# Four fused network layers: the feed-forward's last batch taken by tiles, and sums and boxes of the last stage laid out over its calls

## The chip, the cores and the metric

The kernel is one program on one core of a Trainium2 chip. The core has TensorE (PE in the profile; PEld is its weight load), VectorE (DVE), ScalarE (ACT), GpSimd (POOL), and SyncE (SP), which here only issues transfers. DRAM is reached by DMA from queues on SP, ACT and POOL. The metric is the time of one execution on the device in microseconds, the median of several runs. A measurement of this kernel spreads over some 0.2%. "Span" is the time from the first to the last event in a profiled execution.

## The reference, cut to what matters

The input x has 4 batches of 384 channels on 64 x 64 points. Four layers of the form x = x + layer(norm(x)) follow, where the norm takes groups of 12 channels. Layer 0 is attention, layer 1 a frequency-domain mix, layer 2 a gated block with convolutions and a feed-forward, and layer 3 a depthwise 7 x 7 convolution whose kernels are computed from the input. The change lies in the end of layer 2 and in layer 3:

```
# layer 2, end; _bn is a batch norm with statistics over batch and points
h1 = _gelu(_bn(_pw(tok, cm_w1), cm_g1, cm_b1))      # 384 -> 768 channels
h2 = _bn(_pw(h1, cm_w2), cm_g2, cm_b2)              # 768 -> 384
return gate * (tok + h2) + (1.0 - gate) * x
# layer 3
x_avg, x_max = x.mean(axis=(2, 3)), x.max(axis=(2, 3))
x_w = gelu(x_avg @ w_avg.T + b_avg + x_max @ w_max.T + b_max)
xr = (x_w[:, :, None] * w_mix[None]).reshape(b, c, 7, 7)
Gx = sqrt(sum(xr * xr)); Nx = Gx / (Gx.mean(axis=1) + EPS)
kern = gamma * (xr * Nx) + beta                     # one 7 x 7 kernel per batch and channel
out = depthwise_conv(x, kern)
```

Two facts shape the program. A batch norm needs the statistics of all batches before a single value can be used. And layer 3's kernel is a scalar per batch and channel times w_mix, plus beta everywhere. So the convolution splits into one with the fixed w_mix (weights as Toeplitz matrices, TensorE) and a sum over a 7 x 7 box (the "boxes"). The scalars, called a_s and b_s, need the mean, the largest value and the variance of the whole of layer 3's input (here "x2").

## The kernel before, in words

Channels lie in three tiles j of 128 partitions, and a batch's 4096 points are cut into four blocks or pieces of 1024. A scheduler at compile time puts the program's instructions in order on every engine: it starts from the order in which the Python code emits them, and lets an instruction go ahead if it is ready earlier by a cost model. At run time each engine works its list in order. So the place at which the code emits an instruction decides, but loosely. A named tile of a pool with `bufs=n` rotates over n buffers, and a writer waits until the buffer's last user is done.

**Feed-forward, first half** (lines 1643 to 1699). 768 hidden channels are computed, stored in DRAM (`hidden`), with statistics of each. The sum `wx` of all that x2 has besides h2 is stored too.

**Feed-forward, second half** (lines 1702 to 1739). For each batch b, block i (3 MB of `hidden` into `f_h`, two buffers, GELU in place on ScalarE, line 1722) and tile j, `feed_back` does 12 products of 512 columns (line 1758; every fp32 product is two records in the profile). It copies them out of PSUM on ScalarE (line 1765), takes statistics on DVE (line 1766), and, for j of 1 and 2, stores h2 in DRAM from a rotating buffer `f_h2` (line 1768, POOL's queue). Tile 0's h2 stays in SBUF in `z_`. The loop goes by batch, then block, then tile; only the last batch has one exchange: tile 0 of its last block comes one job sooner. When tile 0 is complete, `h2_norms` computes its factors `gh` and `g0`, and `x2_first` forms x2 = h2 * gh + wx for tile 0 (line 1812) in seven steps ahead of each of the remaining jobs. For batch 3 this is in `z_` with squares and maxima taken at once (lines 1825 and 1827); for batches 0 to 2 it is in three large buffers of 2 MB, `x2_ahead`, into which wx was loaded beforehand. After the last job `h2_norms` does tiles 1 and 2.

**Layer 3** (`phase_g`). `group_means` needs the norms of all tiles. `to_strips` turns tile 0 of x2 around (ScalarE and DVE scale, TensorE transposes in line 2061, ScalarE and DVE copy back in lines 2066 and 2068) into `z_`, all four batches. Then 48 calls of `conv7` follow, 16 for each tile, 8 channels each: four Toeplitz products on DVE or POOL (line 2117), 64 records of matmuls (line 2130) and a copy of the result, stored to `raw` (tiles 0 and 1, line 2145) or added to `rest` and stored to the output (tile 2, lines 2142 and 2147). Other work is cut into steps by Python generators, and a call of conv7, which has five yields, emits a few of them:

- `x2_later`: squares and maxima of tile 0's batches 0 to 2, put behind the strips by `issue_after`.
- `x2_of` (line 2030): x2 of tiles 1 and 2. For each of eight pairs (j, b) it loads 2 MB of wx into one of the same three large buffers, loads h2 by quarters (`g_h`), scales on ScalarE into PSUM with g0 as bias (line 2044), adds on DVE (line 2045), squares, takes the maximum, and stores 2 MB to DRAM. Five steps; two or three a call, all within the first 16 calls.
- `factors`: the chain to a_s and b_s, emitted in one go when tile 0 is convolved, behind all of x2.
- `half_strips`: the strips of the next tile, from DRAM.
- `boxes` (line 2150): for each of twelve pairs (j, b) four parts of three steps each. Sums on POOL and DVE, transposes (line 2208), matmuls (line 2243), the addition into x (line 2245). For tiles 0 and 1 `raw` comes back as `in_raw` (line 2218) and is added: for tile 0 through ScalarE with bias g0 (line 2226) and DVE (line 2229), for tile 1 in one DVE instruction (line 2224). Then the 2 MB of output are stored (line 2233). Tile 2's boxes go to `rest` (line 2235). One step at each of conv7's five yields in tile 1's calls, four or five in tile 2's.

## Time and profile before

| | us |
|---|---|
| median of 5 runs (4696.37 to 4707.07) | 4703.63 |
| the profiled execution's own time | 4706.53 |
| its span | 4704.7 |
| feed-forward, second half: matmuls of line 1758, first to last start | 3512.7 to 4009.1 |
| first convolution (line 2130) | 4051.7 |
| last square of x2 (line 1825) | 4254.4 |
| first box matmul (line 2243) | 4278.7 |
| last convolution ends | 4700.2 |

The page counts busy time of each engine, shows the span in 40 slices with the granted clock of TensorE and the share of time that the 16 DMA engines were busy, and lists groups of instructions by line: busy time, mean of one, idle time of the engine ahead of them and what ended it. A busy share over the whole span (TensorE has 4353.4 us, 93%) says little about the stages in question, so times by stage are used: rows that give, for a stretch, its length, the busy time and the number of instructions of TensorE, its weight load, DVE, ACT and POOL, then the clock, the DMA share and GB/s. A wait is listed as the engine and line that waited, what it waited for, the total in us, how often, and the longest.

### The profile page before, as it was taken

How to read it: one execution, taken by the hardware profiler on the slowest of the kernel's cores; microseconds unless marked ns; L12 is line 12 of the kernel's file. 1: busy time of each engine (PE TensorE's matmuls, PEld its weight loads, DVE VectorE, ACT ScalarE, POOL GpSimd, SP SyncE). 2: the span in 40 equal slices, each digit the busy share in tenths (PEclk: the TensorE clock that was granted, in tenths of full speed). 3: DMA queues.
4: the chain of work that ended last, by engine and by line, in shares of the span. 5: the costliest groups of instructions: out<-in, count | busy, mean ns of one | idle time of the engine just before them, and what ended most of it. 6: DMA issues, size and time to landing. Idle time of an engine off the chain costs nothing. (4 is left out here: it accounts for less than half of the span.)

```text
span 4704.7 us, 49708 instructions
## 1 busy us (share of the span) xinstructions
PE 4353.4 (93%) x18445; PEld 2419.2 (51%) x18445; DVE 2848.9 (61%) x4673; ACT 1966.6 (42%) x2915; POOL 806.3 (17%) x756
## 2 busy tenths in 40 slices
PE   7899999999999999998988999699999999678898
PEld 2233444334443444444548888344444444578888
DVE  6766566645666456545877788655531112867788
ACT  3444344444444444434535666311123333664431
POOL 1000000000000000000025566000000000236665
PEclk9999999999999999998989999799999999888999
DMA  4311222121111211112328999876764333696787
GB/s 138 114 33 50 83 67 74 46 70 47 54 67 56 69 34 61 54 61 82 125 90 290 316 336 325 280 260 246 262 235 161 127 143 136 254 361 229 243 270 260
DMA packets 282128, 730.35 MB, mean 155 GB/s; under 512 B 22059, under 2 KB 122518, under 8 KB 269974
## 3 DMA queue, kind: packets, MB, share of 16 engines
q1 hardware_dynamic: 211336, 407.56, 27.3%
q0 software_dynamic: 38448, 173.96, 9.9%
q10 hardware_dynamic: 32094, 145.57, 7.7%
q8 instruction: 149, 2.44, 0.2%
q14 instruction: 101, 0.83, 0.1%
HBM read 433.13 MB, written 293.86 MB: 155 GB/s over the span
## 5 line engine op out<-in xcount | busy, mean ns | idle before, releaser
L822 ACT ACTIVATE probs<-sc_s 128x1024 f32<-128x1024 f32 x512 | 496.7, 1020 | 689.6 <-PE av L932 588.2
L932 PE MATMUL av<-probs,vt 128*128 128x512 f32 x1536 | 714.9, 602 | 0.0
L1137 DVE SCALAR_TENSOR_TENSOR acc<-band,vecs,acc 128x512 f32<-128x512 f32 x708 | 496.2, 745 | 44.7 <-POOL band L1096 39.6
L1758 PE MATMUL h_m<-f_h,cm_w_t 128*128 128x512 f32 x1152 | 497.0, 594 | 7.4 <-ACT f_h L1722 7.4
L1424 PE MATMUL conv_m<-toep,z 128*128 128x192 f32 (+1 forms) x2304 | 446.7, 351 | 21.7 <-DVE z L1353 12.0
L932 PEld LDWEIGHTS av<-probs,vt 128*128 128x128 f32 x1536 | 275.6, 191 | 338.1 <-issue 334.4
L2130 PE MATMUL conv_m<-toep,z 128*128 128x128 f32 x3072 | 387.9, 284 | 44.7 <-DVE toep L2117 36.2
L1424 PEld LDWEIGHTS conv_m<-toep,z 128*128 128x128 f32 x2304 | 402.6, 194 | 45.7 <-ACT d_o L1435 15.6
L2130 PEld LDWEIGHTS conv_m<-toep,z 128*128 128x128 f32 x3072 | 374.1, 200 | 46.9 <-issue 22.5
L1670 PE MATMUL h_s<-e_tok,cm_w_t 128*128 128x512 f32 x768 | 362.7, 595 | 4.1 <-DVE e_tok L1655 4.1
L1758 PEld LDWEIGHTS h_m<-f_h,cm_w_t 128*128 128x128 f32 x1152 | 219.7, 191 | 284.8 <-issue 274.9
L814 PE MATMUL sc_s<-q,k 32*128 32x512 f32 x2048 | 307.5, 643 | 15.9 <-ACT probs L822 15.6
L1405 POOL TENSOR_TENSOR toep<-w,band 128x1280 f32<-128x1280 f32 x96 | 278.2, 2898 | 200.2 <-PE conv_m L1424 187.8
L1058 PE MATMUL t_m<-w_in_t,xb 128*128 128x384 f32 x768 | 278.4, 497 | 4.6 <-DVE coef L1075 4.4
L968 PE MATMUL proj_m<-xm,w_proj_t 128*128 128x512 f32 x576 | 271.8, 611 | 6.4 <-DVE xm L907 4.9
L1677 ACT COPY e_h<-h_s 128x1024 f32<-128x1024 f32 x96 | 97.2, 1012 | 399.5 <-PE h_s L1670 399.5
L1679 DVE BATCH_NORM_STATS2 h_st<-e_h 128x6 f32<-128x512 f32 x192 | 123.5, 685 | 213.4 <-ACT e_h L1677 213.3
L1670 PEld LDWEIGHTS h_s<-e_tok,cm_w_t 128*128 128x128 f32 x768 | 146.3, 191 | 187.9 <-issue 183.2
L1058 PEld LDWEIGHTS t_m<-w_in_t,xb 128*128 128x128 f32 x768 | 142.7, 192 | 141.6 <-issue 58.8
L975 DVE SCALAR_TENSOR_TENSOR x_res<-proj_m,bn_c,x_res 128x512 f32<-128x512 f32 x96 | 71.8, 748 | 236.4 <-PE proj_m L968 236.2
L1766 DVE BATCH_NORM_STATS2 h_st<-f_h 128x6 f32<-128x512 f32 x64 | 44.2, 693 | 260.7 <-ACT f_h L1765 260.7
L1670 PE MATMUL h_s<-z,cm_w_t 128*128 128x512 f32 x384 | 196.1, 592 | 0.0
(459 smaller groups left out, 6368.3 us busy)
## 6 DMA issues: line engine op xcount, KB each, us to landing
d<-d_o ACTq DMA_DIRECT2D x48, 1024.0 KB
c_d<-d SPq DMA_DIRECT2D x48, 1024.0 KB
hid<-e_h ACTq DMA_DIRECT2D x16, 3072.0 KB
f_h<-hid SPq DMA_DIRECT2D x16, 3072.0 KB
x_in<-in_x SPq DMA_DIRECT2D x96, 256.0 KB
x_res<-in_x SPq DMA_DIRECT2D x32, 768.0 KB
xa<-x_res POOLq DMA_DIRECT2D x32, 768.0 KB, 3.9
xa_out<-xa SPq DMA_DIRECT2D x32, 768.0 KB
```

What stands on the lines that cost most here:

```text
L814: nc.tensor.matmul(s[:, g], lhsT=k4[32 * g : 32 * g + 32, c], rhs=q[i][32 * g : 32 * g + 32], start=True, stop=True,)
L822: nc.scalar.activation(p[:, h * 1024 : (h + 1) * 1024], s[:, 2 * h : 2 * h + 2].rearrange("p a b -> p (a b)"), AF.Exp, scale=0.25,)
L932: nc.tensor.matmul(av[0], lhsT=vt[:, 4 * c + v, :], rhs=p[:, v * 512 : (v + 1) * 512], start=c == 0 and v == 0, stop=c == 7 and v == 3,)
L968: nc.tensor.matmul(m, lhsT=self.w_proj[:, j, o * P : (o + 1) * P], rhs=xm[:, j], start=j == 0, stop=j == NJ - 1,)
L1058: nc.tensor.matmul(m[:, 0:C], lhsT=xb[:, j], rhs=self.w_in[:, j, :], start=j == 0, stop=j == NJ - 1,)
L1137: nc.vector.scalar_tensor_tensor(out, src(j, k), w, done, ALU.mult, ALU.add)
L1405: eng.tensor_tensor(t, self.w53[:, at : at + 160].rearrange("p (m n) -> p m n", n=8).unsqueeze(2).to_broadcast([P, 20, 8, 8]), band.rearra ...
L1424: nc.tensor.matmul(m[:, c * 256 + to : c * 256 + to + 64 * (k1 - k0)], lhsT=self.z_[:, at : at + P], rhs=t[:, 10 * c + k0 : 10 * c + k1].r ...
L1670: nc.tensor.matmul(s[:, v, :], lhsT=w1[:, j, o * P : (o + 1) * P], rhs=t[j][:, v * 512 : (v + 1) * 512], start=j == 0, stop=j == NJ - 1,)
L1679: nc.vector.bn_stats(st[:, o, 8 * b + 2 * i + v, :], h[:, o, v * 512 : (v + 1) * 512])
L1758: nc.tensor.matmul(m, lhsT=w2[:, o, j * P : (j + 1) * P], rhs=h[:, o, v * 512 : (v + 1) * 512], start=o == 0, stop=o == 5,)
L2130: nc.tensor.matmul(m[:, ch % 4 * P : (ch % 4 + 1) * P], lhsT=self.z_[:, at : at + P], rhs=t[:, 8 * c + 2 * i : 8 * c + 2 * i + 2].rearrang ...
```

## The change

The last batch's loop in the feed-forward goes by tile first: all four blocks of tile 0, then of tile 1, then of tile 2. For this all four blocks of its hidden values must be in SBUF: blocks 0 and 1 (12 pieces) go to the three large buffers `x2_ahead`, blocks 2 and 3 to the two buffers of `f_h`. So tile 0's norms come eight jobs ahead of the end. `x2_first` then forms x2 of tile 0 for all batches in `z_`, loading wx by pieces into three small buffers and a spare, with squares (into PSUM) and maxima at once, and stores each batch. Norms of tile 1 follow before the last four jobs, and `x2_second` forms x2 of tile 1, batch 0. When the large buffers have served as hidden values, ScalarE copies tile 0's batches 0 to 2 from `z_` into them (12 copies). `f_h2` has two buffers instead of three.

In layer 3 `x2_later` is gone. `x2_of` has seven pairs, two steps a call, and `factors`, cut by three yields, comes as the last piece of the same list; only when this list is empty do the boxes start, one step at each yield of conv7, through the end. g0 is left out of x2 of tile 1 (bias zero), as it was for tile 0, and the boxes of tile 1 add it through ScalarE like those of tile 0.

```diff
--- before.py
+++ after.py
-            jobs = [(b, i, j) for b in range(B) for i in range(4) for j in range(NJ)]
-            jobs[-4:-3], jobs[-3:-2] = jobs[-3:-2], jobs[-4:-3]
-            tiles, own = {}, iter(())
-            for b, i, j in jobs:
+            tiles = {}
+            def ready(b, i):
+                src = self.hidden[b][:, :, blk].rearrange("o p n -> p o n")
+                if b == B - 1 and i < 2:
+                    h, runs = [], ((0, 4), (4, 2)) if i == 0 else ((0, 2), (2, 4))
+                    for o0, n in runs:
+                        k = 6 * i + o0
+                        t = self.x2_ahead[k // 4][:, k % 4 * 1024 : (k % 4 + n) * 1024].rearrange("p (o n) -> p o n", o=n)
+                        nc.sync.dma_start(t, src[:, o0 : o0 + n])
+                        h += [t[:, o] for o in range(n)]
+                else:
+                    t = hp.tile([P, 6, 1024], F32, tag="h", name="f_h")
+                    nc.sync.dma_start(t, src)
+                    h = [t[:, o] for o in range(6)]
+                for o in range(6):
+                    self.last_gelu = nc.scalar.activation(
+                        h[o], h[o], AF.Gelu, bias=c1[:, o : o + 1], scale=a1[:, o : o + 1]
+                    )
+                tiles[b, i] = h
+            late = B - 1
+            for b in range(late):
+                for i in range(4):
+                    ready(b, i)
+                    if b == late - 1 and i > 1:
+                        ready(late, i - 2)
+                    if b == late - 1 and i == 3:
+                        ready(late, 2)
+                    for j in range(NJ):
+                        self.feed_back(b, i, j, w2, tiles[b, i])
+                    if (b, i) == (0, 0):
+                        self.mix_norms()
+            ready(late, 3)
+            self.ln_exp(self.last_gelu)
+            own = iter(())
+            for j in range(NJ):
+                for i in range(4):
+                    self.feed_back(late, i, j, w2, tiles[late, i])
+                    for _ in range(8):
+                        next(own, None)
+                    if j == NJ - 1 and i < 2:
+                        for b in range(1) if i == 0 else range(1, NJ):
+                            for q in range(4):
+                                at = q * 1024
+                                nc.scalar.copy(
+                                    self.x2_ahead[b][:, at : at + 1024], self.z_[:, b * N + at : b * N + at + 1024]
+                                )
+                self.h2_norms(slice(j, j + 1))
                 if j == 0:
-                    h = hp.tile([P, 6, 1024], F32, tag="h", name="f_h")
-                    tiles[b, i] = h
-                    nc.sync.dma_start(h, self.hidden[b][:, :, blk].rearrange("o p n -> p o n"))
-                    for o in range(6):
-                        last = nc.scalar.activation(
-                            h[:, o, :], h[:, o, :], AF.Gelu, bias=c1[:, o : o + 1], scale=a1[:, o : o + 1]
-                        )
-                    if b == B - 1 and i == 3:
-                        self.ln_exp(last)
-                    if b == B - 1 and 0 < i:
-                        nc.sync.dma_start(self.x2_ahead[i - 1], self.wx[i - 1][:, 0])
-                if (b, i, j) == (0, 1, 0):
-                    self.mix_norms()
-                for _ in range(7):
-                    next(own, None)
-                self.feed_back(b, i, j, w2, tiles[b, i])
-                if (b, i, j) == (B - 1, 3, 0):
-                    self.h2_norms(slice(0, 1))
-                    own = self.x2_first()
+                    first2 = self.x2_first()
+                    own = self.in_turn(first2, self.x2_second())
+                if j == 1:
+                    for _ in first2:
+                        pass
             for _ in own:
                 pass
-            self.h2_norms(slice(1, NJ))
+    def in_turn(self, *pieces):
+        for p in pieces:
+            yield from p
...
-        out = self.io.tile([P, 1024], F32, tag="x", name="f_h2") if j else self.z_[:, at : at + 1024]
+        out = self.io.tile([P, 1024], F32, tag="x", name="f_h2", bufs=2) if j else self.z_[:, at : at + 1024]
...
-            if j:
+            if j == NJ - 1:
-            if j == 0:
+            if j < NJ - 1:
...
     def x2_first(self):
-        for b in (B - 1, 0, 1, 2):
+        for b in range(B):
-                h = self.z_[:, b * N + at : b * N + at + 1024]
-                if b == B - 1:
-                    x = h
-                    other = spare if q % 2 else self.io.tile([P, 1024], F32, tag="wx", name="f_wx", bufs=1)
-                    nc.sync.dma_start(other, self.wx[b][:, 0, at : at + 1024])
-                else:
-                    x = other = self.x2_ahead[b][:, at : at + 1024]
-                nc.vector.scalar_tensor_tensor(x, h, self.gh[:, 0, b : b + 1], other, ALU.mult, ALU.add)
+                x = self.z_[:, b * N + at : b * N + at + 1024]
+                w = self.spare() if q == 3 else self.io.tile([P, 1024], F32, tag="wx", name="f_wx", bufs=3)
+                nc.sync.dma_start(w, self.wx[b][:, 0, at : at + 1024])
+                nc.vector.scalar_tensor_tensor(x, x, self.gh[:, 0, b : b + 1], w, ALU.mult, ALU.add)
                 yield
-                if b == B - 1:
-                    self.x2_piece(0, b, q, x, other)
-                    yield
-            nc.gpsimd.dma_start(self.scratch["x2"][b][0], self.x2_tile(b))
-    def x2_piece(self, j, b, q, x, junk, behind=()):
+                self.x2_piece(0, b, q, x, self.ps("x2_sq").rearrange("p a b -> p (a b)"))
+                yield
+            nc.gpsimd.dma_start(self.scratch["x2"][b][0], self.z_[:, b * N : b * N + N])
+    def x2_second(self):
+        nc = self.nc
+        for b in range(1):
+            for q in range(4):
+                sl = slice(q * 1024, q * 1024 + 1024)
+                x = self.io.tile([P, 1024], F32, tag="wx", name="f_wx", bufs=3)
+                nc.sync.dma_start(x, self.wx[b][:, 1, sl])
+                h = self.spare() if q % 2 else self.io.tile([P, 1024], F32, tag="x", name="f_h2", bufs=2)
+                nc.sync.dma_start(h, self.h2[b][:, 1, sl])
+                nc.vector.scalar_tensor_tensor(x, h, self.gh[:, 1, b : b + 1], x, ALU.mult, ALU.add)
+                yield
+                self.x2_piece(1, b, q, x, self.ps("x2_sq").rearrange("p a b -> p (a b)"))
+                nc.gpsimd.dma_start(self.scratch["x2"][b][1][:, sl], x)
+                yield
-        order = [self.tc.issue_after(e.ins) for e in behind] or [nullcontext()] * 2
-        with order[0]:
-            self.nc.scalar.activation(junk, x, AF.Square, bias=at(self.neg2), accum_out=to(self.x2_var))
-        with order[1]:
-            self.nc.vector.tensor_reduce(to(self.x2_max), x, AX.X, ALU.max)
-    def x2_later(self):
-        for b in range(B - 1):
-            for q in range(4):
-                junk = self.gw_p.tile([P, 1024], F32, tag="w7", name="x2_sq", bufs=3)
-                self.x2_piece(0, b, q, self.x2_tile(b)[:, q * 1024 : q * 1024 + 1024], junk, self.strip_ends)
-                yield
+        self.nc.scalar.activation(junk, x, AF.Square, bias=at(self.neg2), accum_out=to(self.x2_var))
+        self.nc.vector.tensor_reduce(to(self.x2_max), x, AX.X, ALU.max)
...
+            self.zero = cp.tile([P, 1], F32, tag="zero", name="zero")
+            nc.gpsimd.memset(self.zero, 0.0)
...
-            later = self.x2_later()
-            x2 = others(*(self.x2_of(j, b) for j in (1, 2) for b in range(B)))
-            boxes = others(*(self.boxes(j, b) for j, b in ((2, 0), (2, 1), (2, 2), (2, 3), (0, 0), (0, 1), (0, 2), (0, 3))))
-            boxes1 = others(*(self.boxes(1, b) for b in range(B)))
+            x2 = [self.x2_of(j, b) for j, b in ((1, 1), (1, 2), (1, 3), (2, 0), (2, 1), (2, 2), (2, 3))]
+            x2 = self.in_turn(*x2, self.factors())
+            boxes = self.in_turn(*(self.boxes(j, b) for j in (2, 0) for b in range(B)))
+            boxes1 = self.in_turn(*(self.boxes(1, b) for b in range(B)))
             self.load_mix(0)
+            x2_left = True
...
                         for k, _ in enumerate(self.conv7(j, 64 * half + 8 * n)):
                             if k == 0:
                                 next(strips, None)
-                            next(later, None)
-                            if j == 0 and (k < 2 or k == 2 and n % 2):
-                                next(x2, None)
-                            if j == 1 or j == 2 and (k or n % 2):
+                            if x2_left:
+                                if k < 2:
+                                    x2_left = next(x2, "none") != "none"
+                            else:
                                 next(boxes, None)
-                if j == 0:
-                    for _ in x2:
-                        pass
-                    self.factors()
-                    self.pair_scales(2)
                 if j == 1:
-                    boxes = others(boxes, boxes1)
+                    boxes = self.in_turn(boxes, boxes1)
...
-        nc.vector.tensor_sub(self.s_b[:, 0], self.g0[:, 0], m[:, 0])
-        nc.vector.tensor_scalar(self.s_b[:, 1:NJ], m[:, 1:NJ], -1.0, None, ALU.mult)
+        nc.vector.tensor_sub(self.s_b[:, 0:2], self.g0[:, 0:2], m[:, 0:2])
+        nc.vector.tensor_scalar(self.s_b[:, 2:NJ], m[:, 2:NJ], -1.0, None, ALU.mult)
...
+        yield
...
-        nc.vector.tensor_add(mx[:, 0], mx[:, 0], self.g0[:, 0])
+        nc.vector.tensor_add(mx[:, 0:2], mx[:, 0:2], self.g0[:, 0:2])
+        yield
...
+        yield
...
+        self.pair_scales(2)
...
+        bias = at(self.g0) if j == NJ - 1 else self.zero
...
-                nc.scalar.activation(m, h[:, v * 512 : v * 512 + 512], AF.Identity, bias=at(self.g0), scale=at(self.gh))
+                nc.scalar.activation(m, h[:, v * 512 : v * 512 + 512], AF.Identity, bias=bias, scale=at(self.gh))
...
-                if j:
-                    nc.vector.scalar_tensor_tensor(xp, d, self.a_s[:, j, b : b + 1], xp, ALU.mult, ALU.add)
-                else:
-                    nc.scalar.activation(
-                        d, d, AF.Identity, bias=self.g0[:, j, b : b + 1], scale=self.a_s[:, j, b : b + 1]
-                    )
-                    nc.vector.tensor_add(xp, xp, d)
+                nc.scalar.activation(d, d, AF.Identity, bias=self.g0[:, j, b : b + 1], scale=self.a_s[:, j, b : b + 1])
+                nc.vector.tensor_add(xp, xp, d)
```

## The prediction, made before the result was known

> **What bounds the kernel now.** I read the page first: the 40 slices, then the costliest groups. After that I read busy time by stage, the waits inside one stage, and the groups of the lines that the change touches.
>
> The page's span and four of its slice rows (a slice is 117.6 us):
>
> ```profile
> span 4704.7 us, 49708 instructions
> PE   7899999999999999998988999699999999678898
> DVE  6766566645666456545877788655531112867788
> PEclk9999999999999999998989999799999999888999
> DMA  4311222121111211112328999876764333696787
> ```
>
> The reader is to see TensorE at 9 in slices 31 to 34 (the feed-forward), where DVE is at 1 and 2 and DMA at 3. Slices 35 and 36 follow, where TensorE falls to 6 and 7, its clock to 8 and DMA rises to 9. The stages the change touches, one row each: end of the feed-forward, strips of tile 0, x2 with the first convolution, the factors, second third, last third.
>
> ```profile
> core 0: us, PE busy (x) PEld busy (x) DVE busy (x) ACT busy (x) POOL busy (x), PEclk, DMA share, GB/s
> 3886.00:4010.00 124.00, 123.70 (x289) 54.47 (x287) 41.25 (x62) 41.10 (x54) 5.84 (x11) 1.00 0.43 161
> 4010.00:4052.00 42.00, 21.46 (x137) 16.92 (x138) 34.16 (x66) 28.24 (x33) 12.71 (x29) 0.84 0.42 151
> 4052.00:4254.00 202.00, 149.51 (x1186) 146.62 (x1184) 147.29 (x162) 130.28 (x204) 74.95 (x60) 0.87 0.95 343
> 4254.00:4285.00 31.00, 23.14 (x132) 22.80 (x133) 20.03 (x47) 8.95 (x17) 15.34 (x20) 0.61 0.59 215
> 4285.00:4498.00 213.00, 190.07 (x1603) 186.41 (x1603) 165.65 (x211) 87.45 (x132) 141.60 (x135) 0.96 0.75 230
> 4498.00:4705.00 207.00, 186.78 (x1615) 184.06 (x1614) 182.25 (x229) 47.55 (x75) 119.61 (x105) 0.98 0.81 265
> ```
>
> So there are four different limits. The feed-forward is TensorE alone (123.7 of 124). The x2 stage is transfers (share 0.95, 343 GB/s). The factors stage is a chain of short operations, with the clock at 0.61. The last two thirds have TensorE at 89 to 90%, and in the last one DVE has 182 of 207. The waits inside 4051 to 4270 confirm the second:
>
> ```profile
> ACT x_m L2044 <- DMA g_h<-h: 47.5, 18, 6.5
> DVE x L2045 <- ACT x_m L2044: 40.6, 16, 6.5
> PE conv_m L2130 <- DVE toep L2117: 33.2, 8, 10.2
> POOL toep L2117 <- DMA wmix<-in_mix_t: 25.9, 5, 7.3
> ```
>
> ScalarE waits for h2 from DRAM, DVE for ScalarE, and the Toeplitz products behind those adds on DVE reach TensorE late.
>
> Prices:
>
> ```profile
> L1758 PE MATMUL h_m<-f_h,cm_w_t 128*128 128x512 f32 x1152 | 497.0, 594 | 7.4 <-ACT f_h L1722 7.4
> L1812 DVE SCALAR_TENSOR_TENSOR x<-z,gh,x 128x1024 f32<-128x1024 f32 x12 | 14.6, 1271 | 0.0
> L1827 DVE TENSOR_REDUCE x_max<-x 128x1 f32<-128x1024 f32 x44 | 52.6, 1212 | 0.0
> L2224 DVE SCALAR_TENSOR_TENSOR in_x<-in_raw,a_s,in_x 128x1024 f32<-128x1024 f32 x16 | 25.0, 1562 | 7.8 <-DMA in_raw<-raw 7.8
> L2226 ACT ACTIVATE in_raw<-in_raw,g,a_s 128x1024 f32<-128x1024 f32 x16 | 19.9, 1242 | 25.8 <-DMA in_raw<-raw 25.8
> ```
>
> **The change, part by part.** "Piece" means 1024 columns of one tile and batch.
>
> *Feed-forward, order.* The matmuls stay: 1152 records in 497.0 us, 10.3 us per call of feed_back (24 records of 0.43 us). A late block's 3 MB load took 12.6 us from issue (3947.97) to its first GELU, and its six GELUs 7.4 us. Blocks 0 and 1 go to idle buffers and can load at any time. Block 3 is issued when block (2,3) is done and first needed three calls (31 us) later, so 20 us are hidden: 0 us. Without that cover a late block would cost up to 20 us.
>
> *Feed-forward, added work.* Tile 0 ends 8 calls, 82 us, before the end. Into these go 16 + 4 pieces. On DVE each costs 1.27 + 1.21: 20 x 2.48 = 50 us, plus 16 x 0.69 for bn_stats, 61 of 82. On ScalarE there are 20 squares. The row into SBUF has 1.14 + 0.19; into PSUM it is bounded by two halves of the 0.77 us that L2044 takes there, 1.55. I take 1.2 (nearest in size), 28 us. Then 12 copies, between 1.01 (L1677, from PSUM) and 1.24 (L1374, SBUF), 14 us at 1.15, and 16 evacuations of 0.58: 51 of 82. Transfers: h2 4.2 MB, wx of tile 0 8.4, x2 of tile 0 8.4, the quarter 2.1 x 3: 27 MB in 82 us is 333 GB/s, against 343 above, so they fit with little to spare. Half of it is uneven: during tile 1 (41 us) DVE needs 45 us and transfers 19 MB, 55 us at 343, so that some 14 us spill into tile 2, which has 41 us and needs 15 of DVE. POOL's queue carries eight more stores, and h2's stores stand behind those that wait for DVE; f_h2 loses a buffer (3 to 2). Both hold an evacuation back; four PSUM buffers of 5.15 us and two f_h2 of 10.3 cover 41 us. So 0 us; ends -3 (below) and +20, if the spill outlasts tile 2.
>
> The Trainium skill (DMA: Bandwidth & Descriptors, "Issuing engines are not separate DMA queues") speaks against this move: starting transfers from several engines saves only issue time, since they share 16 engines. The same page's fabric ceiling of 435 GB/s would make the 19 MB 44 us, an estimate, and the spill 3 us instead of 14; no stretch here reached it.
>
> *Transition.* Now the last bn_stats starts at 4011.03, behind L1812, though its copy ended 4010.3; two tiles' norms follow until 4016.3. The strips start on ScalarE at 4020.3, when the last h2 store lands (issued 4011.9 behind a 2 MB store of x2, landed 4020.2). With x2 stored earlier and one tile's norms, I put the store's landing at 4018 (its median 7.7 us) and s_b at 4016.5. The strips themselves (30 us, ScalarE) stay. First convolution at 4049 instead of 4051.7: -2.7.
>
> *x2 stage.* Twelve squares and maxima of x2_later go (16 us ScalarE, 14.5 DVE), x2_of falls from 8 to 7, at 6.3 MB each. The first loads of x2_of no longer wait for x2_later's squares to free their buffer: wx was first issued at 4058.4; now at some 4028, bringing 3.7 MB ahead of 4049. Pieces go 2 to a call of conv7, so 28 pieces and their 7 stores end at call 17.5. Until then the transfers are 44.0 - 3.7, plus 17.5 x 0.79 (raw and wmix), strips of tile 1 some 5, one box load 2.1: 61 MB, at 350 GB/s (71 MB in 202 us now) 174 us. Against that TensorE has 17.5 x 64 records x 0.112 plus strips, some 135, DVE some 130. So x2 ends at 4223 rather than 4254.
>
> *Factors.* Three yields set them between calls. Now TensorE spent 31 us at 4254 to 4285 on one and a half calls. After: 1.7 calls at 7.15 us of matmuls and strips, some 12 us. Boxes start at 4235, with call 20 ahead, against 4285 with call 18 ahead. Ends: 4225, 4260 (the stall kept whole).
>
> *Second and last third.* From there 28 calls hold all 144 steps of the boxes, 5 a call; now 30 calls did. Calls 20 to 31: TensorE now has 190.1 us for 14 calls; less two calls (14.3) and 6.7 box parts (at 2.65 us, some 18) 158, at 92% 172 us. Calls 32 to 47 take 27 box parts, now 20. A part costs DVE 1.1 + 2 x 0.74 + 1.56 + 0.60 + 0.70 + 0.34 = 5.8, so 182 + 40 = 222 us, and at the 92% that DVE had in its best 50 us (46.0 busy, the row below) 241 us. TensorE has 205 there: DVE becomes the bound.
> ```profile
> 4600.00:4650.00 50.00, 43.77 (x373) 43.17 (x372) 46.02 (x60) 6.91 (x13) 32.30 (x29) 0.97 0.85 298
> ```
>
> For tile 1, L2224 gives way to L2226 and L2229: DVE equal (1.21 to 1.52 against 1.29 to 1.56), ScalarE 16 x 1.24 = 20 us more, beside only 47.6 busy of 207; its cost is a hop of 1.3 us per part, 0 while DVE has other work. Spreading leaves no spare step, so the last box's sums and its 2 MB store come after the last convolution: 7.9 us to land, as the last of now (4694.2 to 4702.1), where the present end has 0.5 MB.
>
> *Sum.* 4235 + 172 + 241 + 8 = 4656, against the profiled span of 4704.7 (its own time 4706.5, 1.8 around it, 2.9 above the median 4703.6). The difference, -49, on the median: 4655.
>
> **Rivals.**
> Better: DVE doesn't bind, and the 346 us of TensorE work left at 4235 run at the present 90.5%: 382 + 11, from 4225: 4618 in span, 4617. For it: 420 us held 348 of DVE without trouble. Against it: DVE's 92% in 4600 to 4650.
> The early pace stays: calls 0 to 15 took 11.6 us each now (4051.7 to 4237.5). If transfers keep that for 20 calls, boxes start at 4281, and the end comes 46 us later than forecast: 4702 in span, 4701. For it: the strips of tile 1 join the same engines at share 0.95. Against it: 61 MB rather than 71.
> Slower: DVE in the last third works at the share of the second, 78% (165.7 of 213), or less, since in_raw then passes ScalarE first and DVE, in order, waits with Toeplitz products behind. At 78%: 222 / 0.78 = 285, +44, 4699. It turns slower beyond +49, that is below 76.5%; at 72%, 308, 4722. For it: L2229 waited 13.9 us in four places. Against it: 88% in this third now.
> The change does not do what it says: x2 in the feed-forward stalls TensorE by the 20 us above: 4675, still faster.
>
> **How the numbers follow.** 0.2% is 9.4 us, about what a measurement here can tell from no change. Forecast 0.53, of it 0.08 for the stall of 20, own range 4630 to 4680; better 0.21; early pace 0.15; slower 0.11. Faster: 0.53 + 0.21 + 0.05 of the early pace = 0.79; same 0.06, all early pace; slower 0.11 + 0.04 = 0.15. From 4602 (15 under the better case) to 4702 (the early pace) some 0.8 is held.
>
> **What would show it.** Right: TensorE without gaps up to its last h_m; first conv_m within 4 us of 4049; g_h pieces 28, the last by 4225; no stretch of 25 us with the clock near 0.6; box steps spread to the end, DVE over 90% in the last third, a 2 MB store as the last transfer. Wrong: idle time before L1758; the wait for g_h not below 40 us; Toeplitz products late after call 32.

## The result and the profile after

The changed kernel takes 4713.79 us in the median, the kernel before 4704.82, taken alternately on the same chips. The ratio is 1.0015 with a 95% interval of 1.0008 to 1.0022: some 7 us slower, where 4655 us and a gain of 49 were forecast. The time lies above the range given (4630 to 4680).

The profiled execution's own time is 4712.19 us. From the page of the changed kernel, its span and four slice rows (a slice is 117.8 us):

```profile
span 4710.4 us, 49815 instructions
PE   7899999999999999998988899699999999789887
DVE  6766566645566446545877888655531115767787
PEclk9999999999999999998989999799999999889899
DMA  4301212121111111112338999776764335886776
```

VectorE has more work in the feed-forward's last slice (slice 34 at 5, where it was 2). But TensorE ends with 9, 8, 8, 7 where it had 8, 8, 9, 8: time was won in the middle and lost at the end. The stretches of the changed kernel: feed-forward's last part, strips, x2 until its last piece, the factors until call 20, calls 20 to 31, calls 32 to 47 (columns as in the prediction):

```profile
core 0: us, PE busy (x) PEld busy (x) DVE busy (x) ACT busy (x) POOL busy (x), PEclk, DMA share, GB/s
3880.00:4005.00 125.00, 123.58 (x288) 54.34 (x287) 68.33 (x101) 58.24 (x88) 8.99 (x17) 1.00 0.60 227
4005.00:4044.00 39.00, 24.49 (x136) 19.73 (x137) 31.22 (x56) 28.69 (x32) 12.48 (x29) 0.78 0.73 264
4044.00:4228.00 184.00, 152.58 (x1225) 150.09 (x1225) 129.45 (x140) 109.97 (x170) 76.98 (x62) 0.92 0.91 319
4228.00:4264.00 36.00, 32.59 (x229) 32.26 (x228) 22.80 (x43) 12.85 (x20) 15.21 (x16) 0.80 0.67 213
4264.00:4443.00 179.00, 160.14 (x1337) 157.52 (x1337) 131.18 (x171) 66.33 (x104) 116.07 (x115) 0.93 0.63 194
4443.00:4695.00 252.00, 210.71 (x1728) 205.75 (x1726) 206.00 (x267) 79.07 (x108) 135.86 (x125) 0.94 0.76 249
```

The reader is to see three things. In the feed-forward the added VectorE and ScalarE work costs TensorE nothing (123.58 of 125). The x2 stage has transfers at 0.91 and 319 GB/s, less than the 0.95 and 343 of before. And in the last row neither engine is full: VectorE 206 of 252 us (82%), TensorE 84%, where 92% of VectorE was forecast. What stands still there is told by the waits of calls 32 to 47:

```profile
ACT in_raw L2254 <- DMA in_raw<-raw: 67.6, 21, 8.5
PE box_m L2269 <- ACT ht L2241: 35.5, 12, 6.8
DVE in_x L2271 <- PE box_m L2269: 35.2, 15, 7.4
```

ScalarE waits for the transfer in_raw (67.6 us in 21 places), TensorE's box sums wait for ScalarE's copies ht, and VectorE's in_x waits for those sums.

Counted from the first convolution, which takes out how long the stages in front happened to take in a profile, the end comes after 666.6 us; before it was 653.0. So the loss lies behind the first convolution.

### The profile page after: what moved, and what is told of

It is laid out like the page before. It is cut to its first block, busy times and chain, and to the rows that moved or that the text cites. A ratio compares the mean times of both kernels' runs of the same rounds, so it can differ in the third digit from the quotient of the medians.

```text
span 4710.4 us, 49815 instructions
## 1 busy us (share of the span) xinstructions
PE 4365.2 (93%) x18445; PEld 2428.4 (52%) x18445; DVE 2849.9 (61%) x4680; ACT 1991.6 (42%) x2937; POOL 802.9 (17%) x760
## 5 line engine op out<-in xcount | busy, mean ns | idle before, releaser
L1791 PE MATMUL h_m<-f_h,cm_w_t 128*128 128x512 f32 x1008 | 436.4, 595 | 7.4 <-ACT f_h L1728 7.4
L1791 PEld LDWEIGHTS h_m<-f_h,cm_w_t 128*128 128x128 f32 x1008 | 192.5, 191 | 250.8 <-issue 240.0
L968 PEld LDWEIGHTS proj_m<-xm,w_proj_t 128*128 128x128 f32 x576 | 110.5, 195 | 159.5 <-issue 139.1
```

Source lines behind the costliest of these rows:

```text
L968: nc.tensor.matmul(m, lhsT=self.w_proj[:, j, o * P : (o + 1) * P], rhs=xm[:, j], start=j == 0, stop=j == NJ - 1,)
L1791: nc.tensor.matmul(m, lhsT=w2[:, o, j * P : (j + 1) * P], rhs=h[o][:, v * 512 : (v + 1) * 512], start=o == 0, stop=o == 5,)
```

## Experiments

Ratios are to the kernel before, with 95% intervals; a difference of two ratios is turned into us at 4705, and with intervals of this width such a difference is uncertain by 7 to 11 us. A profile is one execution, which can lie some us off the median of its kernel.

### One part at a time

Four kernels split the change into three parts: the feed-forward, the hop (tile 1's raw result through ScalarE) and the spreading (x2 at two steps per call, factors with yields, then boxes at five steps per call).

**Changed kernel without the hop.**

```
# g0 of tile 1 is in x2 again (bias of x2_of, x2_second, s_b, maximum), and
-                nc.scalar.activation(d, d, AF.Identity, bias=self.g0[...], scale=self.a_s[...])
-                nc.vector.tensor_add(xp, xp, d)
+                if j:
+                    nc.vector.scalar_tensor_tensor(xp, d, self.a_s[...], xp, ALU.mult, ALU.add)
+                else: ...   # as it was
```

> The changed kernel, but the raw result of tile 1 is added in one VectorE instruction as before the change (g0 of tile 1 goes into x2 again, in ScalarE's bias where x2 is formed in the convolution stage, and in 4 more ScalarE passes in the feed-forward's last stretch). Theory H (the hop: ScalarE waits for the transfer in_raw at the head of its list, the box transposes' copies ht stand behind it, TensorE's box sums wait for those and VectorE's in_x for these): ScalarE's waits on in_raw in the last third fall from 67.6 us to under 35, TensorE's waits of box_m on ht from 37 to about 20, and the time from 4714 to about 4690 (4680 to 4700). Theory S (the spreading: all box steps run in calls 20 to 47 at five per call with none to spare, at the pace that the conv and box work of one call have together): the waits change places, the time stays at 4706 to 4716.

4698.9 us, 0.9981 (0.9968 to 0.9994): 16 us off the changed kernel, at the slow edge of theory H's range. Its waits came as H said: in calls 32 to 47 ScalarE waits 28.9 us for in_raw (67.6 with the hop), TensorE's box sums 14.6 us for the copies ht (35.5). S is not refuted, since it may hold beside H.

**Feed-forward part alone.**

```
-            x2 = self.in_turn(*x2, self.factors())
+            x2 = self.in_turn(*x2)
...
+                            if j == 0 and (k < 2 or k == 2 and n % 2):
+                                next(x2, None)
+                            if j == 1 or j == 2 and (k or n % 2):
+                                next(boxes, None)
...  # factors in one block after call 15; no hop, as in the run above
```

> The feed-forward part of the change alone: last batch by tiles, two blocks in large buffers, x2 of tile 0 and the first batch of tile 1 formed there; but tile 1's raw result added in one VectorE instruction, the factors in one block after call 15 and the boxes at five and 4.5 steps per call from call 16 on, all as in the kernel before. x2 is then formed by call 14, so nothing of it is left at the end of the first third. If the feed-forward part is worth what it takes off the x2 stage (the factors begin at about 4212 instead of 4254, less the two calls that the kernel before has done by then, 14 us): 4705 - 28 = 4677 (4670 to 4690). If the third third (VectorE) is the limit in both, the gain is given back there: 4695 to 4708.

4669.53 us, 0.9913 (0.9896 to 0.9929): 41 us faster than before. The feed-forward part is worth even more than expected here, and it is not given back.

**Changed kernel without its spreading** (the same edit of the loop, the hop kept).

> The changed kernel without its spreading: feed-forward part and ScalarE's part in tile 1's raw result as changed, factors in one block after call 15 and boxes at five and 4.5 steps per call from call 16, as in the kernel before. If hop and spreading cost apart from one another: 4669.5 + 16 = 4686 (4680 to 4692). If the hop costs only where the steps are packed: 4667 to 4675.

4681.93 us, 0.9953 (0.9935 to 0.9970). The hop costs 19 us here (against 0.9913), so not only where the steps are packed.

**The hop alone, on the kernel before.**

```
-                if j:
-                    nc.vector.scalar_tensor_tensor(xp, d, self.a_s[...], xp, ALU.mult, ALU.add)
-                else: ...
+                nc.scalar.activation(d, d, AF.Identity, bias=(self.zero if j else self.g0[...]), scale=self.a_s[...])
+                nc.vector.tensor_add(xp, xp, d)
```

> The kernel before, with one thing of the change alone: the raw result of tile 1 goes through ScalarE (scale a_s, bias zero) and then a VectorE addition, as tile 0's, instead of one VectorE instruction. It adds 16 x 1.24 = 20 us to ScalarE. Theory H (the hop costs by itself): ScalarE's waits on in_raw rise from 23 us to about 50 and the time from 4705 to about 4722 (4715 to 4735). Theory S (the hop costs only because the steps are packed at five per call): 4702 to 4710.

4724.68 us, 1.0026 (1.0008 to 1.0043): 12 us slower. So the parts are: feed-forward -41 us (0.9913), hop +12, +16 and +19 (three pairs), spreading +32 (0.9981 against 0.9913, without the hop) and +29 (1.0015 against 0.9953, with it). That -41 + 19 + 29 gives the +7 of the result is no test, since these kernels form a chain from the one before to the changed one. The test is that the hop costs about the same in three surroundings and the spreading in two: within the uncertainty each has its price whether the other is there or not. Counted from the first convolution, single profiles give 20, 22 and 8 us for the hop and 20 and 34 for the spreading, so the prices are known to some 10 us.

Calls 32 to 47 show the hop by itself. The rows of the feed-forward part alone, and of the same with the hop:

```profile
4464.10:4665.90 201.80, 187.95 (x1616) 185.41 (x1614) 180.81 (x228) 47.77 (x75) 117.92 (x103) 0.97 0.79 268
```

```profile
4457.20:4672.80 215.60, 192.97 (x1616) 189.66 (x1614) 183.66 (x228) 66.46 (x91) 117.96 (x103) 0.95 0.76 250
```

ScalarE has 19 us more work (16 instructions), VectorE 3 more, and the stretch is 13.8 us longer. The waits in the same two stretches, without and with the hop:

```profile
ACT in_raw L2260 <- DMA in_raw<-raw: 8.3, 4, 4.2
PE box_m L2277 <- ACT ht L2244: 13.2, 7, 3.9
DVE in_x L2279 <- PE box_m L2277: 7.6, 5, 3.9
```

```profile
ACT in_raw L2258 <- DMA in_raw<-raw: 59.5, 18, 9.0
PE box_m L2273 <- ACT ht L2245: 22.6, 10, 6.9
DVE in_x L2275 <- PE box_m L2273: 17.0, 8, 6.7
```

The transfer's issue was held back without the hop too: SyncE, which issues it, waited 81 us in front of it in these calls, and 95 with the hop. That cost little while VectorE met tile 1's late transfers (its wait for in_raw is 8.5 us). With the hop the waits of all three engines grow, by 51, 9 and 9 us.

### Why in_raw is late for ScalarE

Three runs tried to take that wait away.

```
# the transfer two box steps earlier; its issue further down is taken out
+            if j < NJ - 1:
+                d = ...; nc.sync.dma_start(d..., self.raw[j]...)
             yield
             for q in range(2):
```

> The changed kernel, but each in_raw transfer is issued two box steps earlier (before the box transposes instead of after the last box sum of its part), so that it has landed when ScalarE comes to it; all else stays, the two instructions per part of tile 1 too. Theory H: ScalarE's waits on in_raw fall from 67.6 us to under 30 and the time to about 4688 (4678 to 4700). Theory S: 4706 to 4716. Against both: in_raw shares three buffers with the convolution's results (rest_o), and a transfer that holds one longer can make ScalarE's or VectorE's evacuation of the convolution wait; then 4715 to 4740.

4715.06 us, 1.0015 (1.0001 to 1.0029); the wait on in_raw stays at 67.6 us. SyncE's queue says why it did not come sooner; its waits in the changed kernel, calls 32 to 47:

```profile
SPq L2249 <- DVE in_x L2255: 44.0, 9, 10.4
SPq L2140 <- DVE in_x L2255: 43.5, 14, 8.5
SPq L2249 <- DMA out<-rest_o: 41.6, 10, 8.5
SPq L2178 <- DVE rest_o L2173: 34.8, 12, 8.6
```

The issue of in_raw (L2249) stands in one list with the load of `rest` (L2140) and the output's store (L2178), and waits for a buffer that in_x's addition or an output's store has to give back. So the next run had five buffers:

```
-  tag="rest", name="in_raw", bufs=3      (and rest_o)
+  tag="rest", name="in_raw", bufs=5
...  # the gate's weights go into other buffers, to make the room
```

> The changed kernel with five buffers instead of three for rest_o and in_raw (the gate's weights are loaded into three box_7 buffers when the factors begin, which makes the room). In the run with the earlier issue, in_raw did not come earlier: SyncE's queue waits for a buffer (in the changed kernel in_raw waits 44.0 us for in_x's additions and 41.6 for rest_o's stores, the load of rest another 43.5). Theory B (the hop costs by holding one of three shared buffers longer): those waits fall under a third, ScalarE's waits on in_raw from 67.6 us to under 25, and the time from 4714 to about 4692 (4682 to 4700). Theory O (the hop costs by the order on ScalarE, whatever the buffers): in_raw comes earlier, but the time stays at 4708 to 4716.

4709.91 us, 1.0009 (0.9998 to 1.0021); the wait on in_raw is 66.3 us, and `rest`'s load now waits 68.8 us for in_x. Theory B falls, since its buffers did not bring the transfer sooner; for the same reason this is no test of theory O. Then the addition itself was put behind the next part's copies:

```
             if q == 0: ...
+            if left:
+                self.add_raw(j, b, *left)     # ScalarE's and VectorE's instruction
             yield
...
+                left = (x[:, part * 1024 : (part + 1) * 1024], d)
```

> The changed kernel, but the addition of a part's raw result (ScalarE's and VectorE's instruction, tiles 0 and 1) comes two box steps after its transfer is issued, behind the next part's two copies ht, so that ScalarE does not stand before in_raw with those copies behind it (the last part of a box keeps its place). Theory Q (the hop costs by what is queued behind ScalarE's wait): ScalarE's waits on in_raw in calls 32 to 47 fall from 67.6 us to under 30, TensorE's of box_m on ht from 35.5 to under 20, and the time from 4713 to about 4699 (4690 to 4704), that of the kernel with one VectorE instruction. Theory T (it costs by its 20 us of ScalarE and the longer way of one buffer, whatever stands behind it): 4707 to 4716.

> The same on the changed kernel without its spreading (4682 us; 4669.5 with one VectorE instruction for tile 1). Theory Q: 4670 (4664 to 4676), the waits on in_raw from 59.5 us to under 30. Theory T: 4679 to 4686.

On the changed kernel 4713.52 us, 1.0025 (1.0011 to 1.0039); without its spreading 4675.92 us, 0.9938 (0.9914 to 0.9962) against 0.9953, which the intervals don't tell apart. But the waits on in_raw stayed at 69.4 and 49.7 us: the edit did not take away what it was meant to. So it tells nothing against theory Q. That the hop costs 12 to 19 us is shown; that it does so by what stands behind ScalarE's wait, and not by its own 19 us of ScalarE or by holding a buffer longer, is argued from the waits. It also stays open which holder of the buffers or of SyncE's list would have to move for the transfer to come in time.

### What of the spreading costs

**x2 at 2.5 steps per call**, alone and with the hop taken out:

```
-                                if k < 2:
+                                if k < 2 or k == 2 and n % 2:
```

> The changed kernel, but x2 is formed at 2.5 steps per call as before the change instead of 2, so that factors and boxes are handed out from about call 16 instead of 20, and 16 to 20 steps are to spare at the end. Theory S (too many box steps on too few calls): x2 ends at about the same time, with 3 to 4 calls fewer done, the calls from there to the end cost some 14 us instead of 15.4, the tail after the last convolution shrinks from 16 us to 5, and the time falls to about 4695 (4688 to 4702). Theory H (the hop): the same waits of ScalarE on in_raw, 60 us or more in the last third, and the time stays within 5 us of 4714, but for what the tail gives back.

> Both edits at once: tile 1's raw result added in one VectorE instruction, and x2 at 2.5 steps per call. Theory H: as with the first edit alone, about 4690. Theory S: as with the second alone, about 4695. If both causes are real and add: about 4672 (4662 to 4684).

4704.03 us, 0.9991 (0.9978 to 1.0005), and 4690.98 us, 0.9964 (0.9952 to 0.9976). Against the same kernels at two steps per call these are 11 and 8 us less, and for the second pair the intervals overlap. The tail behind the last convolution is 4.6 us instead of 15.9, so in the first run the tail alone is the gain, as theory H allowed; theory S's 4695 was missed, and ScalarE still waits 60.7 us for in_raw in calls 32 to 47. The second run lies 19 us above the 4672 that was forecast if both causes add. **Five buffers on top of both**:

> Five buffers for rest_o and in_raw on top of tile 1's addition in one VectorE instruction and x2 at 2.5 steps per call (that took 4691 with three buffers, and SyncE waited there still 35 us for in_x and 40 for rest_o's stores before in_raw). Theory B: another 10 us, 4681 (4672 to 4686). Theory O: 4688 to 4694, as with three.

4690.9 us, 0.9969 (0.9956 to 0.9982): no change that can be told, the time that theory O gave.

The run with both edits now has factors and boxes at nearly the same calls as the feed-forward part alone, and is still 24 us behind it (0.9964 against 0.9913). Four differences were taken one by one.

**4.5 box steps in the last third**, `elif j < 2 or k or n % 2: next(boxes, None)`:

> The kernel with both edits (one VectorE instruction for tile 1's raw result, x2 at 2.5 steps per call; 4691 us, boxes from call 15.6 at five steps per call), but in the last third 4.5 box steps per call, as the kernel before. Theory P (place in the call: at five per call the raw additions fall beside GpSimd's box sums and take 1.92 us instead of 1.38 to 1.54, 32 of them, 13 us on VectorE): the raw additions come back to 1.55 or less in the last third and the time falls to about 4678 (4668 to 4685). Theory R (the rate matters by itself: fewer steps beside each call let VectorE feed TensorE): the same. Against both: 4688 to 4694, then it is the two steps by which the boxes start earlier, or the factors.

**Feed-forward part alone, five steps in the last third**, `if j: next(boxes, None)`:

> The feed-forward part alone (4669.5 us), but five box steps per call in the last third too, as the change has it, instead of 4.5. Theory R or P (five per call cost VectorE more beside GpSimd's work): 4680 to 4692. If the rate does not matter and the start of the boxes does: 4666 to 4674.

**Feed-forward part alone, factors spread over calls 14 and 15:**

> The feed-forward part alone (4669.5 us), and of the spreading one thing: the factors are handed out with yields behind the last piece of x2, in calls 14 and 15, instead of in one block after call 15. The boxes keep their place and rate. Theory F (spreading the factors is worth the stall that TensorE has there, 41 us for calls 16 and 17 against 34 with the spread factors of the run with both edits): 4662 (4655 to 4667). Theory D (how the box steps fall beside GpSimd's work decides; factors cost the same wherever they are): 4667 to 4673.

**Both edits, boxes from call 16 exactly**, two steps later, `if x2_left:` becoming `if j == 0:`:

> The kernel with both edits (tile 1's raw result added in one instruction, x2 at 2.5 steps per call, boxes from the fourth step of call 15 on; 4691 us), with the boxes begun at call 16 instead, two steps later. Theory P (place): the raw additions fall from 1.92 us mean to about 1.55 and the time to about 4672 (4664 to 4680). Theory L (the number of calls that the boxes have): two steps later is no better, 4688 to 4694.

Measured: 4670.47 us, 0.9926 (0.9906 to 0.9946); 4672.21, 0.9928 (0.9905 to 0.9951); 4665.01, 0.9909 (0.9893 to 0.9926); 4667.63, 0.9922 (0.9905 to 0.9938). Five steps per call cost nothing that can be told where the boxes start at call 16 and the factors are one block (0.9928 against 0.9913, the intervals overlap), and spreading the factors wins nothing that can be told (0.9909). The start two steps later is worth 20 us (0.9964 against 0.9922); 4.5 steps are worth 18 at the earlier start, and they too move the steps to other places. VectorE's two forms of raw addition, in the run with both edits and in the one two steps later:

```profile
L2259 DVE TENSOR_TENSOR in_x<-in_x,in_raw 128x1024 f32<-128x1024 f32 x16 | 30.9, 1934 | 11.9 <-ACT in_raw L2256 11.9
L2254 DVE SCALAR_TENSOR_TENSOR in_x<-in_raw,a_s,in_x 128x1024 f32<-128x1024 f32 x16 | 30.6, 1915 | 1.9 <-DMA in_raw<-raw 1.9
```

```profile
L2254 DVE SCALAR_TENSOR_TENSOR in_x<-in_raw,a_s,in_x 128x1024 f32<-128x1024 f32 x16 | 26.6, 1663 | 6.0 <-DMA in_raw<-raw 6.0
L2259 DVE TENSOR_TENSOR in_x<-in_x,in_raw 128x1024 f32<-128x1024 f32 x16 | 25.0, 1562 | 14.5 <-ACT in_raw L2256 14.5
```

The same 32 instructions take 61.6 us in one place and 51.6 in the other. That is theory P's mechanism with half of its 20 us. In the profiles most of the difference lies in calls 20 to 31, here in the run with both edits and in the one two steps later:

```profile
4285.10:4475.80 190.70, 163.43 (x1338) 160.21 (x1337) 139.04 (x172) 71.30 (x108) 113.32 (x104) 0.93 0.71 224
```

```profile
4282.30:4461.70 179.40, 157.91 (x1338) 155.24 (x1338) 132.79 (x174) 71.22 (x108) 114.13 (x107) 0.95 0.73 233
```

VectorE has 6 us more work there, and its in_x waits 29.0 us for the box sums instead of 16.8. The four kernels whose boxes start in call 15 take 190.7 to 194.5 us for these calls, all others 172.6 to 187.6. Why the sums come later in that place stays open. In the changed kernel the 32 additions take 45.2 us, so their place is not what made the change slow. Whether the place matters there was asked by shifting the boxes of the run without the hop by one and two steps:

```
+                            elif pause:
+                                pause -= 1       # pause = 1, then 2
                             else:
                                 next(boxes, None)
```

> The changed kernel with tile 1's raw result added in one instruction (4699 us, boxes from the third step of call 19 on), with the boxes one step later. Theory P: the place decides, and the three places in turn give different times; one of the two shifted runs lies at 4685 or below. Theory L: 4699 to 4704 for both, a step more behind the last convolution (2 us).

> As the run before, with the boxes two steps later. Theory P: this or the run with one step at 4685 or below. Theory L: 4700 to 4706.

4694.04 us, 0.9980 (0.9969 to 0.9990) and 4693.98 us, 0.9979 (0.9968 to 0.9990), against 0.9981: no place is better, as theory L said. The times lie below its ranges, but the kernel before was faster on that chip too (4703.1 against 4707.4). With x2 at two steps per call and the boxes from call 19 it is 0.998 in all three places; with x2 at 2.5 it is 0.992 with the boxes from call 16 and 0.996 with the boxes two steps earlier. So the slower pace, with the later start that comes of it, costs between 8 us (not clear of noise) and 28 us, by the place that it is compared with. Is earlier still better? Three steps per call, boxes from call 14:

> The kernel with both edits and boxes from call 16 (4668 us), with x2 at three steps per call and the boxes from call 14. Theory L (the earlier the boxes start, the fewer of them are left beside the last calls): 4655 (4645 to 4664). Against it: the transfers have 0.97 of the time already in calls 0 to 15, so x2 cannot end earlier in time and the first 14 calls only take longer: 4664 to 4674.

4674.54 us, 0.9939 (0.9920 to 0.9959): no, nothing that can be told from 0.9922. The 14 calls take 171.3 us, with the transfers at 0.96 and 349 GB/s in the first 160.7 us of that; x2 ends some 149 us after the first convolution, hardly sooner than at 2.5 steps (153 to 162).

The stretches show what happened. Calls 0 to 15 and 16 to 19 of the changed kernel, then of the feed-forward part alone:

```profile
4043.80:4206.70 162.90, 136.93 (x1091) 134.64 (x1092) 113.18 (x123) 97.78 (x150) 61.12 (x46) 0.92 0.92 320
4206.70:4263.80 57.10, 48.22 (x362) 47.71 (x361) 38.96 (x61) 25.24 (x41) 30.87 (x33) 0.85 0.75 252
```

```profile
4045.70:4211.90 166.20, 139.06 (x1093) 136.84 (x1093) 123.27 (x142) 104.89 (x163) 70.65 (x57) 0.89 0.97 343
4211.90:4284.80 72.90, 63.60 (x493) 62.11 (x492) 51.74 (x81) 26.07 (x42) 45.86 (x51) 0.87 0.53 178
```

Sixteen calls take 162.9 us with 32 steps of x2 and 166.2 with all 35. Over all profiles it is 161.2 to 166.2 us in the seven kernels with two steps per call, and 162.7 to 166.2 in the four with 2.5 and the factors behind call 15. Fewer steps per call bought nothing that can be told; TensorE is idle for a sixth of that time in either case. At call 20 the changed kernel is 19 us ahead (220.0 against 239.1), but 17 box steps behind: it has done 3, the other 20. That is nearly six parts, 33 us of VectorE at the 5.8 us a part of the prediction, and they fall on the calls at the end. Without the hop, calls 32 to 47 of the spread kernel hold 80 box steps:

```profile
4459.80:4692.70 232.90, 207.87 (x1727) 202.99 (x1726) 208.13 (x266) 60.15 (x92) 135.43 (x125) 0.95 0.80 270
```

They took 232.9 us with VectorE busy 208.1; with 64 steps, in the feed-forward part alone (the row further up), they took 201.8 and 180.8. The last of the steps stand behind the last convolution. DVE's and POOL's timelines of the changed kernel, at the end:

```profile
4699.23 0.75 DVE L2271 SCALAR_TENSOR_TENSOR in_x<-box_m,b_s,in_x 128x512 f32<-128x512 f32 x1 [1.57 <-PE box_m L2269]
4700.07 1.23 DVE L2255 TENSOR_TENSOR in_x<-in_x,in_raw 128x1024 f32<-128x1024 f32 x1
```

```profile
4702.26 0.59 POOL L2259 DMA_DIRECT2D out<-in_x  x1 [20.00 <-DVE in_x L2255]
```

The last convolution ends at 4694.5, this store lands at 4708.8 and the span ends at 4710.4.

## Why the prediction was wrong

Two steps failed: the spreading was entered as a gain and costs about 30 us (29 and 32 in two pairs), and the hop was entered as 0 and costs 12 to 19. By the terms of the sum, as far as the profile tells:

- *Feed-forward, order and added work, 0 us*: right. From the start of the first product of `feed_back` to the end of the last it took 497.7 us, before 497.0. The added transfers raised the mean of its last part from 161 to 227 GB/s and held nothing back.
- *Transition, -2.7*: from the end of the last product to the first convolution 40.2 us against 42.0, so -1.7. That the first convolution starts at 4043.8, earlier than the 4049 forecast, is for the rest the start of the feed-forward, 6.8 us earlier in this profile (3505.9 against 3512.7), where nothing was changed.
- *x2 stage, 174 us*: 184. The quantity of transfers was not the limit. At two steps per call x2 is handed out no faster than the calls go, and the transfers ran at 319 GB/s instead of the 350 of the forecast (61 MB at the 343 of its own row would be 178 us). With 2.5 steps they ran at 343 and x2 ended 153 to 162 us after the first convolution.
- *Factors, 12 us, boxes from 4235*: this is the term that was off most. From the last piece of x2 (4227.7) to call 20 (4263.8) it took 36 us, and 41 from 4223, where the forecast had x2 end. TensorE's groups in 4223 to 4264:

```profile
L2161 PE MATMUL conv_m<-toep,z 128*128 128x128 f32 x144 | 21.0, 310 | 0.0
L1980 PE MATMUL xw_m<-g_max,w_gate 128*128 128x4 f32 x18 | 5.0, 348 | 0.0
L1980 PE MATMUL xw_m<-g_avg,w_gate 128*128 128x4 f32 x18 | 4.9, 342 | 2.8 <-DVE g_max L1974 2.8
L2042 PE MATMUL strip_m<-ident,ax 128*128 128x128 f32 x29 | 4.5, 309 | 5.5 <-ACT z L2049 5.5
```

  I had counted 1.7 calls, where 2.5 were left (17.5 to 20), and left out the gate's own products (the two xw_m rows, 7.4 us from the first to the next convolution), the first boxes and the two waits. The clock in the middle of it was 0.53 (4242 to 4250). So call 20 began 29 us later than forecast. The end kept whole, 4260, was the better number.
- *Calls 20 to 31, 172 us*: 179.2.
- *Calls 32 to 47, 241 us, VectorE at 92%*: 251.5, at 82%. Without the hop 232.9, at 89%. VectorE's load was put too high (206 busy, 222 forecast: the stretch holds 27 parts, but before it held 64 steps, 21 parts, not 20), and its share too high; these two errors work against each other, so it is luck that the term is off by 10 only. What failed was the sentence that the hop costs "0 while DVE has other work": in this stretch it cost 18.6 us in one pair and 13.8 in the other, and 12 to 19 in the whole time. By the waits, VectorE, which works its list in order, stands at the in_x behind a late ht.
- *Tail, 8 us*: 15.9. The store took 6.5 us (4702.3 to 4708.8). I had left out what stands before it: the last part's transposes, copies, sums and addition behind the convolution, 6.8 us (4694.5 to 4701.3).

The terms from the first convolution on are thus off by +34 (x2 and factors), +7, +10.5 and +8, against -5 for its start: 54 us, which is 4710.4 against 4656.

What was right is the part of most weight: forming x2 in the feed-forward costs nothing there and is worth 41 us. What was wrong at the root is that I priced the spreading as a gain. It moves 17 box steps to later calls, and I let the convolution run ahead for it at a pace (174 us for 17.5 calls) that it did not have (184). The rival "slower" named the hop's mechanism, with 78% of VectorE and 4699; measured were 82%. "The early pace stays" (4701) forecast boxes from 4281; the first box product came at 4262.5. The result is made of two rivals that I had kept apart, each in part (29 of the 46 us, 10.5 of the 44), and the tail. Of the prediction's own signs, the first convolution (4043.8, not within 4 us of 4049) and VectorE's share spoke against it; the wait for g_h (33.9 us, under 40) and the 2 MB store at the end came as it said.

## A version that beats both

The feed-forward part with factors spread over calls 14 and 15, boxes from call 16 at five, then 4.5 steps per call, and tile 1's raw result added in one VectorE instruction takes 4665.01 us, 0.9909 (0.9893 to 0.9926). Without spread factors it is 4669.53, 0.9913; these two are not told apart. The second of them is the feed-forward part of the change without its hop and its spreading.

## What to carry to other kernels

Work handed out in steps beside a loop can lose by a slower rate: here it freed nothing, since the main engine was idle for a sixth of the time in either case, and what started late was left over for the calls in which another engine was short. An instruction moved to an idle engine is not free for that engine's idle time: look at what stands behind it in that engine's list and who waits for those results. Shifting interleaved work by two steps changed 20 us here, so vary the place before reading a cause out of one such pair. When a change has several parts, measure each alone: here one was worth 41 us and two others cost 48.

## What the runs showed of the hardware

The VectorE addition of a raw result, 128 x 1024 with both large inputs in SBUF, takes 1.21 to 1.29 us when GpSimd does nothing at that time (5 to 13 of the 32 in each profile), and up to 3.4 us beside a Toeplitz product of GpSimd. In the run with both edits, VectorE's and GpSimd's timelines:

```profile
4434.71 3.05 DVE L2259 TENSOR_TENSOR in_x<-in_x,in_raw 128x1024 f32<-128x1024 f32 x1 [1.79 <-ACT in_raw L2256]
```

```profile
4434.34 2.34 POOL L2147 TENSOR_TENSOR toep<-wmix,band 128x1024 f32<-128x1024 f32 x1
```

The addition begins 0.37 us after the product and ends 1.08 us after it: it looks as if it had waited for the product to end and then run alone (spans of GpSimd are rough in a profile). In the twenty profiles 240 such additions began while a tensor_tensor of GpSimd had more than 0.2 us to go, and 237 of them ended 1.05 to 1.14 us after it. The Trainium skill (SBUF — State Buffer, "Who interferes with whom") says that a VectorE instruction with two SBUF inputs contends with a GpSimd instruction that reads SBUF, and that whichever issues second is held up until the first is done. These rows agree. The prediction had taken 1.56 us for it, a mean over both cases. So a shift by two steps changed 10 us of VectorE's time without any change in its work; nearly half of that is one addition of 6.09 us (at 4635.32 in the run with both edits), which two Toeplitz products of GpSimd overlapped one after the other.
